# Two normalized convolution layers: prologue loads moved from SyncE's queue to GpSimd's, and memsets cut to the columns that stay

## The chip, the cores and the metric

The kernel runs on one core of a Trainium2 chip. A core has five engines that run side by side, each through its own instructions in order: TensorE (PE, matrix products), VectorE (DVE), ScalarE (ACT), GpSimd (POOL) and SyncE (SP). They meet through semaphores. DMA transfers between the chip's main memory (HBM) and the on-chip memory (SBUF) are issued by an engine and carried out by 16 DMA engines. In this kernel SyncE issues nearly all transfers, so its queue is a program of its own, in which a transfer that must wait holds back all that stand behind it.

The metric is the device time of one execution in microseconds. The kernel before takes 3223.17 us (median of 3 runs, 3222.82 to 3223.66).

## The reference

Input x has 4 images of 16 channels, 256 x 256, in float32. Two layers follow each other, and each adds its result to its input:

```python
# layer 0
h = group_norm(x)                                  # 8 groups of 2 channels, over H and W
logits = conv3x3(h, conv_w) + conv_b               # 16 -> 16*25 channels
w = softmax(logits.reshape(4, 16, 25, 256, 256), axis=2)
x = x + sum over the 25 offsets of (h shifted by the offset, zero outside) * w
# layer 1
g = group_norm(x)
base_w = base_weight.sum(axis=2)
spl_w  = (spline_weight * spline_scaler[..., None]).sum(axis=2)
x = x + conv3x3(silu(g), base_w) + conv3x3(b_splines(g), spl_w) + bias
```

So layer 0 is a 5 x 5 filter whose 25 weights differ at each pixel and channel and come from a 3 x 3 convolution. Layer 1 is a 3 x 3 convolution of nine functions of each value: silu and eight cubic B-splines.

## The kernel before, in words

The kernel has three stages.

**Prologue** (0 to about 132 us). It loads the 4 images, half an image (128 rows) at a time, 2 MB each (`load_x`, L408). The two halves of image 0 stay in SBUF (`held`), the other six go through three buffers (`xin`), so that a load waits until the half three before it has been read. For each half VectorE takes statistics (L519, L521), ScalarE squares it (`xq`, L528), and TensorE sums the squares over the channels (L531), which is for a bound on the logits. After both halves of an image, `group_stats` turns the statistics into mean and reciprocal deviation; the power -1/2 is taken on GpSimd (`rstd`, L152). Weights come in too: `wr` and `wnr` for layer 0 (L416 to L428), and for layer 1 `sw` (27 loads, L435), `ss` (3, L437) and `bw` (1, L442). `prepare0` sorts layer 0's weights into `wm` and `wp` (copies on GpSimd, L460 and L461). `prepare1` sums layer 1's weights (L483 to L498).

While images 1 to 3 are still being measured, image 0 is normalized: the generator `normalize` writes h to HBM in three layouts. `hs` holds rows in strips of 32 columns for the weighted sum. `hst` holds columns for the convolution's im2col, and `hsl` the same split into a rounded part and a rest (`hi` and `lo`). ScalarE makes the rows (`hsp`, L312, and `ht`, L325), TensorE transposes (L347), VectorE and ScalarE copy the transposed tiles out (`tt`, `hi`, `lo`, L340 to L355), and SyncE stores them (`put_rows` L273, `put_columns` L287). First of all `normalize` writes zeros around h: 4 stores to `hs` (L245) and 8 to `hst` and `hsl` (L251, L252). All of these are SyncE transfers, in the order in which the scheduler placed them: x loads, `wr`, `wnr`, then `sw`, `ss`, `bw`, the zeros, and only then the stores of h with the remaining x loads between them.

Tiles for `normalize` are made by `norm_tiles`, which zeroes them whole on GpSimd (L226, L228). What must be zero in them are only the borders: two columns at either side of `xp`, and the outermost column of `tt`, `hi` and `lo`. The rest is written over before it is read.

At the end of the prologue VectorE writes a flag that says whether the logits can't overflow, and each engine branches on it.

**Layer 0** (about 132 to 2290 us). A loop over 64 strips of 32 columns, each in steps of four columns: SyncE loads `am` and `an` (im2col of h, L628 and L638) and `u` (h's rows, L652). TensorE makes the logits (L775, L779), ScalarE the exponentials (L798), GpSimd multiplies by h (L803) and VectorE sums numerator and denominator (L680). `normalize` of the next image runs between the steps with tiles of its own, which `norm_tiles` zeroes again. The three `an` tiles are zeroed whole by VectorE first, and two of their rows (64 and 96) then set to one (L613, L615). Rows 64 and 96 carry the bias (its rounded part and the rest); rows 0 to 63 are loaded anew for each use, and the weights that rows 65 to 95 meet are zero.

**Layer 1** (about 2290 to 3222 us). ScalarE and VectorE evaluate the functions, TensorE convolves.

Two rules set the order of work around the change. Within the prologue a scheduler orders each engine's instructions. And transfers use eight completion counters in turn for each kind of issuing queue, so a transfer waits until the one eight before it has landed.

Of the kernel before, what the change touches and what calls it, by code (L numbers as in the profile page):

```python
# [11 lines left out]
F32 = mybir.dt.float32  # L12
# [21 lines left out]
def conv_preact_kernel(  # L34
# [12 lines left out]
    nc = tc.nc  # L47
    B, C, H, W = x.shape
# [3 lines left out]
    NH = H // P  # L52
# [3 lines left out]
    PAD = K // 2  # L56
# [10 lines left out]
    RP = P + 2  # L67
# [16 lines left out]
    hst = [[dram.tile([C, CT], F32, name=f"hst{b}_{h}") for h in range(NH)] for b in range(B)]  # L84
# [30 lines left out]
    KT = 6 * C + 1  # L115
# [17 lines left out]
    def group_stats(pool, psum, st, name):  # L133


        mv = pool.tile([P, G, 2], F32, name=f"mv_{name}", tag="mv")
        for g in range(G):
            nc.vector.bn_aggr(mv[:, g, :], st[:, g].rearrange("p n s -> p (n s)"))
        mps = psum.tile([P, G], F32, name=f"mps_{name}", tag="qp")
        nc.tensor.matmul(mps, lhsT=ones, rhs=mv[:, :, 0], start=True, stop=True)  # L140
        mean = pool.tile([P, G], F32, name=f"mean_{name}", tag="mean")
        nc.vector.tensor_copy(mean, mps)
        d = pool.tile([P, G], F32, name=f"d_{name}", tag="d")
        nc.vector.tensor_sub(d, mv[:, :, 0], mean)
        nc.vector.tensor_mul(d, d, d)
        nc.vector.tensor_add(d, d, mv[:, :, 1])
        vps = psum.tile([P, G], F32, name=f"vps_{name}", tag="qp")
        nc.tensor.matmul(vps, lhsT=ones, rhs=d, start=True, stop=True)
        var = pool.tile([P, G], F32, name=f"var_{name}", tag="var")
        nc.vector.tensor_scalar(var, vps, EPS, None, ALU.add)  # L150
        rstd = pool.tile([P, G], F32, name=f"rstd_{name}", tag="rstd")
        nc.gpsimd.tensor_tensor(rstd, var, mhalf, ALU.pow)  # L152
        return mean, rstd
# [63 lines left out]
    def norm_tiles(prep):  # L217


        xps = [prep.tile([P, QC, W + 2 * PAD], F32, name=f"xp{h}", bufs=1) for h in range(NH)]  # L220
        tts, his, los = [
            [prep.tile([P, NH, QG, RP], d, name=f"{v}{n}", bufs=1) for n in range(2)]
            for v, d in (("tt", F32), ("hi", F32R), ("lo", F32R))
        ]
        for t in (*tts, *xps):
            nc.gpsimd.memset(t, 0.0)  # L226
        for t in (*his, *los):
            nc.gpsimd.memset(t.bitcast(F32), 0.0)  # L228
        return prep, xps, tts, his, los

    zero = const.tile([PAD * C, max(RP, NST * SP)], F32, name="zero")
# [2 lines left out]
    zpad = const.tile([P, QC, PAD], F32, name="zpad")  # L234
    nc.vector.memset(zpad, 0.0)

    def normalize(b, ptr, tiles, held=None, copier=None):

        prep, xps, tts, his, los = tiles
        copier = copier or nc.scalar.copy
        for e in (0, HP - PAD):
            for r in range(PAD):
                nc.sync.dma_start(  # L245
                    hs[b][:, e + r].rearrange("s c w -> c s w"),
                    zero[0:C, 0 : NST * SP].rearrange("c (s w) -> c s w", s=NST),
                )
        for h in range(NH):
            for w in (0, (W + 1) * RP):  # L250
                nc.sync.dma_start(hst[b][h][:, w : w + RP], zero[0:C, 0:RP])  # L251
                nc.sync.dma_start(  # L252
                    hsl[b][h][:, :, w : w + RP].rearrange("c t r -> (c t) r"), zero[:, 0:RP]
                )

# [116 lines left out]
        for q in range(C // QC):  # L372
            ahead = rows(q + 1) if q + 1 < C // QC else iter(())
# [15 lines left out]
    with tc.tile_pool(name="prep0", bufs=2) as prep, tc.tile_pool(  # L389
# [5 lines left out]
    ) as pstat, tc.tile_pool(name="ptr0", bufs=3, space=PSUM) as ptr0:  # L395

        tiles = norm_tiles(prep)
        held = [pre.tile([P, C, W + 2 * PAD], F32, name=f"held{h}") for h in range(NH)]

        def load_x(n):  # L400
            b, h = divmod(n, NH)
            if b == 0:
                t = held[h][:, :, PAD : PAD + W]
                nc.gpsimd.memset(held[h][:, :, 0:PAD], 0.0)
                nc.gpsimd.memset(held[h][:, :, PAD + W :], 0.0)
            else:
                t = xin.tile([P, C, W], F32, name=f"xin_{n}", tag="xin")
            nc.sync.dma_start(t, x[b, :, h * P : (h + 1) * P, :].rearrange("c p w -> p c w"))  # L408
            return t
# [4 lines left out]
        for dj in range(3):  # L414
            v = conv_wt[dj].rearrange("(d c) n -> c d n", d=3)
# [5 lines left out]
        v = conv_wt[2, 2 * C : 3 * C]  # L421
# [8 lines left out]
        sw = pre.tile([P, 3, 9, nm], F32, name="sw")  # L430
        ss = pre.tile([P, 3, 9, nm], F32, name="ss")
        for d in range(3):
            dc = slice(d * C, (d + 1) * C)
            for k in range(9):
                nc.sync.dma_start(sw[:, d, k], spl_w[dc, k])  # L435
            v = spl_s[dc]
            nc.sync.dma_start(  # L437
                ss[:, d],
                bass.AP(tensor=v.tensor, offset=v.offset, ap=[v.ap[0], [0, NS], [1, 9 * nm]]),
            )  # L440
        bw = pre.tile([nm, 9, nm], F32, name="bw")
        nc.sync.dma_start(bw, base_w)  # L442

        ups = pstat.tile([P, 1], F32, name="ups", tag="hps")
        nc.tensor.matmul(
# [64 lines left out]
        ahead = iter(())  # L510
        for b in range(B):
            st = stat.tile([P, G, NH * (GC if b == 0 else 1), 6], F32, name=f"st0_{b}", tag=f"st0{min(b, 1)}")
            for hf in range(NH):
                n = b * NH + hf
                t = loaded.pop(0)
                for g in range(G):
                    if b == 0:
                        for k in range(GC):
                            nc.vector.bn_stats(st[:, g, hf * GC + k, :], t[:, g * GC + k, :])  # L519
                    else:  # L520
                        nc.vector.bn_stats(  # L521
                            st[:, g, hf, :],
                            t[:, g * GC : (g + 1) * GC, :].rearrange("p c w -> p (c w)"),
                        )
                    next(ahead, None)
                    next(ahead, None)

                nc.scalar.activation(xq, t, AF.Square)  # L528
                sq = pstat.tile([P, W], F32, name=f"sq_{n}", tag="sq")
                for c in range(C):  # L530
                    nc.tensor.matmul(  # L531
                        sq, lhsT=idr, rhs=xq[:, c], start=c == 0, stop=c == C - 1
                    )
                nc.vector.tensor_reduce(hm[:, n : n + 1], sq, AX.X, ALU.max)
                next(ahead, None)
                if n >= NH and n + 3 < B * NH:
                    loaded.append(load_x(n + 3))
            mean, rstd = group_stats(stat, pstat, st, f"x{b}")
            nc.vector.tensor_copy(nrm[b][:, 0], rstd)
            nc.vector.scalar_tensor_tensor(nrm[b][:, 1], mean, -1.0, rstd, ALU.mult, ALU.mult)  # L540
            ms = stat.tile([P, 2], F32, name=f"ms_{b}", tag="ms")
            nc.vector.tensor_mul(mean, mean, mean)
            nc.vector.tensor_reduce(ms[:, 0:1], mean, AX.X, ALU.add)
            nc.vector.tensor_scalar(ms[:, 0:1], ms[:, 0:1], 9.0 * GC, None, ALU.mult)
            nc.vector.tensor_reduce(ms[:, 1:2], rstd, AX.X, ALU.max)
            nc.vector.tensor_mul(ms[:, 1:2], ms[:, 1:2], ms[:, 1:2])
            v = hm[:, b * NH : (b + 1) * NH]
            nc.vector.tensor_scalar(v, v, 9.0 / 8.0, ms[:, 0:1], ALU.mult, ALU.add)
            nc.vector.tensor_scalar(v, v, ms[:, 1:2], None, ALU.mult)
            if b == 0:  # L550
                prepare0()
            if b == 1:
                prepare1()
            if b == 0:
                ahead = normalize(0, ptr0, tiles, held, nc.vector.tensor_copy)
                next(ahead)
        for _ in ahead:
            pass
# [39 lines left out]
    def layer0(shift):  # L598
# [4 lines left out]
        with tc.tile_pool(name=f"prep{arm}", bufs=2) as prep, tc.tile_pool(  # L603
# [5 lines left out]
        ) as plog, tc.tile_pool(name=f"prc{arm}", bufs=1, space=PSUM) as prc:  # L609
            ans = [imp.tile([KT, CI * RP], F32R, name=f"an{n}{arm}", bufs=1) for n in range(NIM)]  # L610
            for t in ans:
                v = t.bitcast(F32)
                nc.vector.memset(v, 0.0)  # L613
                for r in (4 * C, 6 * C):
                    nc.vector.memset(v[r : r + 1], 1.0)  # L615
            tiles = norm_tiles(prep)
            strips = [(b, hf, s) for b in range(B) for hf in range(NH) for s in range(NST)]
            nci = SW // CI
# [120 lines left out]
            ahead = iter(())  # L739
            for n, (b, hf, s) in enumerate(strips):  # L740
                if (hf, s) == (0, 0):
                    for _ in ahead:
                        pass
                    ahead = normalize(b + 1, ptr, tiles) if b + 1 < B else iter(())
# [12 lines left out]
                for j in range(0, SW, JG):  # L757
                    if j % CI == 0:
                        k = n * nci + j // CI
# [11 lines left out]
                    for j1 in range(0, JG, 2):  # L771
# [12 lines left out]
                        if shift:  # L784
                            mx = l0.tile([P, 2, C], F32, name=f"mx_{n}_{j}_{j1}{arm}", tag="mx")
                            for i in range(2):
                                v = lg[:, i, :NL].rearrange("p (m c d) -> p m c d", m=K, c=C)
# [3 lines left out]
                                w = bass.AP(  # L791
                                    tensor=mx.tensor, offset=mx.offset + i * C,
                                    ap=[mx.ap[0], [0, K], [1, C], [0, K]],
                                )
# [285 lines left out]
```

## Time and profile before

| what | value |
|---|---|
| time, median of 3 | 3223.17 us |
| prologue, to SyncE's last store of h | 0 to 132.2 us |
| its DMA traffic | 35.3 MB, mean 268 GB/s |
| busy over the whole span: DVE, PE, ACT, POOL | 96%, 89%, 69%, 60% |
| first product e*u of layer 0 (GpSimd) | 145.0 us |

The page's busy shares are over all three stages and hide the prologue, which is 4% of the span. It is best read by stretches: which engine is busy in it, and how much the DMA engines move. The DMA traffic of the prologue in 40 slices of 3.3 us (each digit is the busy share in tenths, below it GB/s):

```profile
DMA  0999999999512323241899999994999999999999
GB/s 5 324 350 348 349 349 348 349 348 348 157 30 38 97 41 91 40 122 26 260 257 348 347 371 284 347 314 182 354 366 297 349 342 365 335 368 332 372 375 376
```

The engines are full until slice 10, little used until slice 18 (about 60 us), and full again to the end.

### The profile page before, as it was taken

What the parts mean: (1) busy time and instruction counts of PE and PEld (TensorE: products, weight loads), DVE (VectorE), ACT (ScalarE), POOL (GpSimd) and SP (SyncE); (2) the same over time, 40 slices, a digit from 0 to 9 for tenths busy, and PEclk for the clock granted to TensorE, in tenths of its full rate; (3) what the DMA queues carried; (4) which work ended last, traced back from release to release, by engine and by line L of the source; (5) the groups of instructions that cost most, each with busy time, mean ns of one, the idle gap of its engine ahead of it and who ended that gap; (6) DMA issues with size and microseconds to landing.
All of it is one profiled execution on the core that took longest, in us unless ns stands there. A gap on an engine that the chain in (4) does not pass through costs nothing. (4 is left out here: it accounts for less than half of the span.)

```text
span 3222.0 us, 40428 instructions
## 1 busy us (share of the span) xinstructions
PE 2862.3 (89%) x14776; PEld 1490.7 (46%) x14776; DVE 3101.7 (96%) x1799; ACT 2208.0 (69%) x2233; POOL 1936.4 (60%) x659
## 2 busy tenths in 40 slices
PE   3499999999999999999999989859999989988988
PEld 3366665666566566656656656512222222222222
DVE  6589999999999999999999999999999999999997
ACT  6366555466554465554444444589999999999996
POOL 2299999999999999999999999900000000000000
PEclk7699999999999999999999999979999999999999
DMA  7988886778877788877756756678878778888883
GB/s 224 291 223 236 229 221 187 212 211 230 246 208 192 203 219 225 249 198 203 210 156 170 191 157 170 163 169 183 178 168 179 180 171 168 180 176 173 178 179 71
DMA packets 356531, 626.34 MB, mean 194 GB/s; under 512 B 45298, under 2 KB 222692, under 8 KB 340452
## 3 DMA queue, kind: packets, MB, share of 16 engines
q1 hardware_dynamic: 323300, 606.88, 75.3%
q10 hardware_dynamic: 33024, 16.78, 1.9%
q8 instruction: 121, 1.98, 0.3%
q14 instruction: 86, 0.70, 0.1%
HBM read 513.95 MB, written 104.24 MB: 192 GB/s over the span
## 5 line engine op out<-in xcount | busy, mean ns | idle before, releaser
L775 PE MATMUL lg<-wm,am 128*128 128x400 f32 x4096 | 1748.9, 508 | 123.4 <-ACT e L798 109.7
L803 POOL TENSOR_TENSOR e<-e,u 128x1600 f32<-128x1600 f32 x512 | 1789.1, 3536 | 68.5 <-ACT e L798 68.0
L680 DVE TENSOR_REDUCE nd<-e 128x128 f32<-128x3200 f32 x512 | 1747.5, 3477 | 23.3 <-POOL e L803 23.2
L798 ACT ACTIVATE e<-lg 128x800 f32<-128x800 f32 x1024 | 815.7, 836 | 896.5 <-DVE nd L680 768.9
L779 PE MATMUL lg<-wn,an 97*128 97x400 f32 x2048 | 1358.4, 663 | 0.5 <-DMA an<-hsl 0.5
L775 PEld LDWEIGHTS lg<-wm,am 128*128 128x128 f32 x4096 | 766.3, 194 | 450.1 <-ACT e L798 161.3
L961 PE MATMUL yp<-ring,wt 128*32 128x512 f32 x6144 | 755.1, 604 | 146.0 <-DVE ring L164 110.4
L779 PEld LDWEIGHTS lg<-wn,an 97*128 97x128 f32 x2048 | 390.8, 191 | 311.9 <-issue 15.6
L961 PEld LDWEIGHTS yp<-ring,wt 128*32 128x32 f32 x6144 | 206.5, 110 | 685.1 <-issue 477.9
L889 POOL MEMSET sx<- 16x256 f32 x8 | 2.4, 303 | 765.6 <-DMA out_dram<-yo 706.6
L977 PE MATMUL yp<-sl,ws 64*32 64x512 f32 x1536 | 176.5, 588 | 0.0
L164 DVE TENSOR_TENSOR ring<-ta,ta 128x2048 f32<-128x2048 f32 (+1 forms) x64 | 147.8, 2309 | 2.5
L164 DVE TENSOR_TENSOR ring<-tb,tb 128x2048 f32<-128x2048 f32 x64 | 145.6, 2276 | 2.6
L163 DVE TENSOR_TENSOR ta<-ta,ta 128x2048 f32<-128x2048 f32 (+1 forms) x64 | 147.3, 2301 | 0.0
L163 DVE TENSOR_TENSOR tb<-tb,tb 128x2048 f32<-128x2048 f32 x64 | 146.5, 2289 | 0.0
L908 ACT ACTIVATE sl<-sx,q 64x2048 f32<-64x2048 f32 x64 | 133.3, 2083 | 0.0
L160 ACT ACTIVATE ta<-ta 128x2048 f32<-128x2048 f32 (+1 forms) x64 | 122.3, 1911 | 0.0
L160 ACT ACTIVATE tb<-tb 128x2048 f32<-128x2048 f32 x64 | 120.5, 1883 | 0.6 <-POOL sx L889 0.6
L193 POOL TENSOR_TENSOR rstd<-rstd,mhalf 128x8 f32<-128x8 f32 x4 | 8.7, 2176 | 175.6 <-DVE rstd L191 175.6
L706 POOL TENSOR_TENSOR xc<-xc,nd 128x512 f32<-128x512 f32 x64 | 98.8, 1544 | 12.1 <-DVE nd L700 12.1
L977 PEld LDWEIGHTS yp<-sl,ws 64*32 64x32 f32 x1536 | 48.8, 106 | 116.2 <-issue 113.2
L923 ACT ACTIVATE xta<-xta,q 128x2048 f32<-128x2048 f32 (+2 forms) x44 | 91.6, 2083 | 0.0
(174 smaller groups left out, 2131.9 us busy)
## 6 DMA issues: line engine op xcount, KB each, us to landing
am<-hst SPq DMA_DIRECT2D x512, 194.6 KB
u<-hs SPq DMA_DIRECT2D x320, 288.0 KB
an<-hsl SPq DMA_DIRECT2D x512, 129.8 KB
xta<-x1s SPq DMA_DIRECT2D x40, 1024.0 KB
xtb<-x1s SPq DMA_DIRECT2D x40, 1024.0 KB
xtc<-x1s SPq DMA_DIRECT2D x40, 1024.0 KB
am<-hst SPq DMA_DIRECT2D x256, 129.8 KB
sx<-x1s SPq DMA_DIRECT2D x248, 128.0 KB
```

The lines of the kernel that those rows point to most:

```text
L160: nc.scalar.activation(s1, r1, AF.Square, scale=2.0)
L163: nc.vector.tensor_mul(s1, s1, r1)
L164: nc.vector.tensor_add(f, s2, s1)
L680: nc.vector.tensor_reduce(nd[:, :, j : j + JG, :], e.rearrange("p t j m c d -> p t j c m d"), AX.XY, ALU.add,)
L706: nc.gpsimd.tensor_sub(v, v, nd[:, 1].rearrange("p j c -> p c j"))
L775: nc.tensor.matmul(lg[:, i, :NL], lhsT=am[:, o : o + P], rhs=wm.rearrange("p m c d -> p (m c d)"), start=True, stop=False,)
L779: nc.tensor.matmul(lg[:, i, :NL], lhsT=an[:, o : o + P], rhs=wn.rearrange("p m c d -> p (m c d)"), start=False, stop=True,)
L798: nc.scalar.activation(ev, lg[:, :, :NL], AF.Exp)
L803: nc.gpsimd.tensor_tensor(e[:, 1].rearrange("p j m c d -> p j (m c) d"), e[:, 0].rearrange("p j m c d -> p j (m c) d"), uv, ALU.mult,)
L908: nc.scalar.activation(sl[n % 2][:, :, 1 : W + 1], t, AF.Silu, scale=sc[b][0][0 : RD * C], bias=sc[b][1][0 : RD * C],)
L961: nc.tensor.matmul(yp[t * M : (t + 1) * M], lhsT=wt[:, d, e].rearrange("p r o -> p (r o)"), rhs=ring[:, r0 + t * RT + d : r0 + t * RT + d ...
L977: nc.tensor.matmul(yp[t * M : (t + 1) * M], lhsT=ws[:, e].rearrange("p r o -> p (r o)"), rhs=sl[n % 2][:, t : t + NT + 1 : NT, e : e + W], ...
```

## The change

Three things are changed. (1) The loads of layer 1's weights (`sw`, `ss`, `bw`) and, for image 0 alone, the zeros around h are issued by GpSimd instead of SyncE. This is to free SyncE's queue for the stores of h and the x loads behind them. (2) `norm_tiles` zeroes only the border columns that no later write covers. (3) The `an` tiles are not zeroed and then given rows of ones; one memset sets rows 64 to 96 to one, since the loads cover rows 0 to 63 and the weights of rows 65 to 95 are zero. Parts 2 and 3 shorten GpSimd's and VectorE's memsets.

```diff
-        for t in (*tts, *xps):
-            nc.gpsimd.memset(t, 0.0)
-        for t in (*his, *los):
-            nc.gpsimd.memset(t.bitcast(F32), 0.0)
+        for t in xps:
+            nc.gpsimd.memset(t[:, :, 0:PAD], 0.0)
+            nc.gpsimd.memset(t[:, :, PAD + W :], 0.0)
+        for t in (*tts, *his, *los):
+            t = t if t.dtype == F32 else t.bitcast(F32)
+            nc.gpsimd.memset(t[:, 0, :, 0:1], 0.0)
+            nc.gpsimd.memset(t[:, NH - 1, :, RP - 1 :], 0.0)
...
-    def normalize(b, ptr, tiles, held=None, copier=None):
+    def normalize(b, ptr, tiles, held=None, copier=None, queue=nc.sync):
...
-                nc.sync.dma_start(
+                queue.dma_start(
                     hs[b][:, e + r].rearrange("s c w -> c s w"),
...
-                nc.sync.dma_start(hst[b][h][:, w : w + RP], zero[0:C, 0:RP])
-                nc.sync.dma_start(
+                queue.dma_start(hst[b][h][:, w : w + RP], zero[0:C, 0:RP])
+                queue.dma_start(
                     hsl[b][h][:, :, w : w + RP].rearrange("c t r -> (c t) r"), zero[:, 0:RP]
...
-                nc.sync.dma_start(sw[:, d, k], spl_w[dc, k])
+                nc.gpsimd.dma_start(sw[:, d, k], spl_w[dc, k])
             v = spl_s[dc]
-            nc.sync.dma_start(
+            nc.gpsimd.dma_start(
                 ss[:, d],
...
-        nc.sync.dma_start(bw, base_w)
+        nc.gpsimd.dma_start(bw, base_w)
...
-                ahead = normalize(0, ptr0, tiles, held, nc.vector.tensor_copy)
+                ahead = normalize(0, ptr0, tiles, held, nc.vector.tensor_copy, nc.gpsimd)
...
-                v = t.bitcast(F32)
-                nc.vector.memset(v, 0.0)
-                for r in (4 * C, 6 * C):
-                    nc.vector.memset(v[r : r + 1], 1.0)
+                nc.vector.memset(t.bitcast(F32)[4 * C : KT], 1.0)
```

## The prediction
> **What bounds the kernel now.** I read the page's 40 slices first: GpSimd and VectorE are full from slice 3 to about slice 28 (layer 0's loop), ScalarE and VectorE after it (layer 1). The diff touches neither loop; it touches the 132 us before them and the first 10 us of the loop. So the second view is busy time by stretch, cut at the points where the SyncE queue changes its work. Columns: stretch, length, busy time of each engine with its instruction count, granted clock, mean DMA share, GB/s.
>
> ```profile
> core 0: us, PE busy (x) PEld busy (x) DVE busy (x) ACT busy (x) POOL busy (x), PEclk, DMA share, GB/s
> 0.00:30.00 30.00, 9.67 (x42) 9.11 (x43) 24.83 (x77) 12.99 (x9) 9.95 (x22) 0.99 0.97 308
> 30.00:62.00 32.00, 18.45 (x81) 14.27 (x80) 20.73 (x64) 30.63 (x41) 7.10 (x13) 0.66 0.39 98
> 62.00:132.00 70.00, 20.95 (x95) 18.02 (x94) 43.79 (x123) 35.38 (x66) 3.28 (x2) 0.57 1.02 327
> ```
>
> The DMA engines are full, then idle six tenths of the time for 32 us, then full for 70 us. ScalarE is the reverse: 30.6 us busy of 32 in the hole, half idle after it. The timeline of the SyncE queue says why (start, length, queue, line, transfer, count):
>
> ```profile
> 35.89 5.70 SPq L435 DMA_DIRECT2D sw<-in_spl_w_dram  x9
> ...
> 56.72 1.85 SPq L245 DMA_DIRECT2D hs<-zero  x4
> ...
> 62.38 1.01 SPq L273 DMA_DIRECT2D hs<-hsp  x2
> 63.49 1.30 SPq L408 DMA_DIRECT2D xin<-in_x_dram  x1
> ```
>
> From 35.9 to 62.4 SyncE issues 43 small transfers, about 0.6 us each. Behind them stand the first stores of h (ready since 34.7 and 38.5, when ScalarE ended hsp) and the sixth x load (its buffer had been read by 33). The chain of waits up to 132 us shows who pays:
>
> ```profile
> DVE st L521 <- DMA xin<-in_x_dram: 13.3, 3, 8.6
> ...
> ACT xq L528 <- DMA xin<-in_x_dram: 11.2, 3, 4.8
> ...
> ACT hsp L312 <- DMA hs<-hsp: 4.9, 2, 4.2
> ```
>
> The x loads of batches 2 and 3 are late. The last one sets the end: its square is the row below at 108.1, and from there to SyncE's last put (131.6) it is a chain of statistics, flag and the last column tiles.
>
> ```profile
> 108.11 3.62 ACT L528 ACTIVATE xq<-xin 128x4096 fp32r<-128x4096 f32 x1 [4.18 <-DMA xin<-in_x_dram]
> ```
>
> GpSimd is idle for most of this, with two rows that matter:
>
> ```profile
> 28.79 1.66 POOL L152 TENSOR_TENSOR rstd_x<-var_x,mhalf 128x8 f32<-128x8 f32 x1 [19.49 <-DVE var_x L150]
> ```
> ```profile
> 30.82 0.87 ACT L312 ACTIVATE hsp<-held,nrm 128x576 f32<-128x576 f32 x1 [1.78 <-DVE ms L545]
> ```
>
> The reciprocal deviation of batch 0 runs on GpSimd the moment its variance is there, and 0.4 us later ScalarE starts normalizing. Everything ScalarE does from 30.8 on hangs on that row.
>
> **What the Trainium skill says.** (1) "DMA: Bandwidth & Descriptors", section "Issuing engines are not separate DMA queues": transfers of all issuing engines interleave on the same 16 DMA engines, so another issuer saves only issue time. No transfer of GpSimd's is in this trace, so it can't confirm that; but it shows issue time being the limit between 36 and 62 (DMA share 0.39). (2) "Perfetto Trace Analysis", section "DMA Instruction — SWDGE (GPSIMD)": a transfer issued by GpSimd has its descriptors written by GpSimd's own cores, and the instruction lasts until they are written. So an issue costs GpSimd engine time, in order with its other work. Not shown here. (3) "SBUF — State Buffer", section "Who interferes with whom": GpSimd and a VectorE copy in its two-port mode lock each other out. The trace agrees: the 16x128 copy of sel takes 6.23 us at 3.15, until GpSimd's memsets end near 9.3.
>
> **The change part by part.**
>
> Memsets at the start. Eight of 128x1040 took 7.4 us of GpSimd (1.75 to 9.05). Sixteen narrow ones replace them; the four 128x32 of held start 0.06 us apart, so about 1 us, and GpSimd is free at 3.0 instead of 9.3. By itself worth nothing: its next work was at 28.8, and the sel copy that it frees isn't needed until layer 1.
>
> Memsets at the start of layer 0. The eight on GpSimd (137.0 to 144.35) end before the first product e*u, which starts at 145.03 and waits 0.68 us for ScalarE. The nine of VectorE (130.0 to 140.5) become three; their only reader on the path, the an load at 135.55, had been waiting 0.3 us. VectorE's first reduce starts at 148.6, after the first product. Value: 0 to 0.3 us.
>
> SyncE's queue. Removed: 31 loads and 12 zero stores, 26.5 us of issue. The queue goes from wnr straight to the hs store. That store waits for the landing of the transfer eight before it on SyncE's rotating completion counters, the fifth x load; that landed at about 35.9, and now shares the DMA engines with the moved loads. These took 8 us of full DMA time in the hole (share 0.31 and 0.33 over 40 to 60, and a little either side), so I take 43. The first store can go at 43 instead of 62.4.
>
> GpSimd's queue, the cost. In the changed program's instruction order, GpSimd issues 27 sw, 3 ss, bw, 4 hs and 1 hst, 36 transfers, *ahead of* the batch 0 reciprocal. Waiting behind them: the reciprocal, then all of ScalarE's normalizing, then SyncE's stores. The trace doesn't show what one such issue costs. Below: SyncE's own rows, 0.597 us for sw, 0.46 for hs zeros, 0.43 for a 16-row one. Above: the 2.0 us fixed cost of a whole GpSimd transfer ("DMA: Bandwidth & Descriptors", section "Anatomy of one DMA — SWDGE (gpsimd) path"), which would hold only if nothing overlapped. I take SyncE's rows scaled by 1.0/0.6, the ratio of first-byte latencies that the same page gives for the two paths ("Latency and other measured facts"): an estimate of 1.0 us for 128-row transfers, 0.77 and 0.72 for the zeros. Waits for the transfer eight before hardly bind at that rate, as eight issues last 8 us.
> 31 x 1.0 + 4 x 0.77 + 0.72 = 34.8; from 3.0 that is 37.8; plus 1.66 for the reciprocal and 0.4 to ScalarE: normalizing starts at 39.9, not 30.8, 9.1 us late.
> What else queues: seven zeros (5.0), sw*ss (2.97), the copies to wm and wp (2.1) end near 49.6. ScalarE's cast of wp comes some 17 us of its work after 39.9, so that hides.
>
> Now the end. ScalarE was busy 55.7 us between 30.8 and the last square at 108.1 (30.6 in the hole, about 25 from 62 on) and waited 21 us, mostly for what SyncE issued late. With SyncE open those waits go. I leave 4 us of them, twice the rate of the hole (1.4 in 32). Last square: 39.9 + 55.7 + 4 = 99.6, 8.5 earlier. Its x load is there: from the first hs store to its issue took 36.4 us (62.4 to 98.8) and 9.3 to land; from 44 that is 89.7. DMA work also fits: the full 70 us from 44 end at 114, while the prologue would end at 131.6 - 8.5 = 123. The loops behind it only shift. Rounding off 0.3 us for slower x loads in the first 40 us: 3223.2 - 8.2 = 3215.
>
> **The rivals.** All hang on the same unknown, c, the issue time of a 128-row transfer on GpSimd.
> A. Forecast, c near 1.0: 3215.
> B. Cheap issue, c of 0.6 to 0.75: the reciprocal is hardly late (24 to 29), and the DMA engines become the bound; end at 114 to 116, 16 us saved: 3207. For it: the transfers are tiny (24 KB). Against it: software writes their descriptors.
> C. Cancels, c near 1.25: normalizing starts at 48.6, the last square at 108.3: 3223. For it: the same arithmetic with one number a quarter larger. Against: zeros with few rows are likely cheaper.
> D. The other side: a new wait takes the place of the old one. At c = 1.5, 52.2 us of issue, start at 57.3, last square at 117, 9 us later: 3232. At 2.0: 69.6, 74.7, 134: 3249. For it: every batch's reciprocal is on GpSimd, and the x loads fill the DMA engines until 36, so landings may be slow and the eight-counter wait may bind. Against: SyncE's x loads leave room between packets if the queues take turns.
>
> **How the numbers follow.** A 0.42, B 0.20, C 0.18, D 0.20. Predicted time is A's. The range leaves out the cheapest end of B and most of D past c = 1.6: 3205 to 3234. Faster than 3216.7: B and seven tenths of A, 0.49. Within 0.2%: the rest of A and most of C, 0.29. Slower than 3229.6: D and a sliver of C, 0.22.
>
> **What would show it.** In the changed kernel's timeline: GpSimd's queue issuing sw from about 3 us at about 1 us each; the first reciprocal near 38 rather than 28.8 and waiting for the queue, not for VectorE; the first hs store near 44; the sixth x load right behind it; the last square near 100; DMA share above 0.8 between 44 and 120; the first logits near 130 instead of 138.9. I am wrong if the reciprocal is after 48 (D), if it is before 32 (B), or if the last square stays near 108 while the reciprocal is early, since then ScalarE's waits were not SyncE's doing.

## The result and the profile after

| kernel | median, us | lowest to highest | runs |
|---|---|---|---|
| before | 3222.99 | 3222.45 to 3223.66 | 4 |
| changed | 3209.85 | 3207.31 to 3210.43 | 4 |

The ratio is 0.9958, 95% interval 0.994 to 0.9975: 13.1 us faster, where 8.2 were forecast. A later series gave 0.9962 (0.9948 to 0.9975). Line numbers move by one to three: L435 of before is L438 here, L528 is L531.

Busy time by stretch of the changed kernel, with the cuts of the prediction's first view (columns as there):

```profile
core 0: us, PE busy (x) PEld busy (x) DVE busy (x) ACT busy (x) POOL busy (x), PEclk, DMA share, GB/s
0.00:30.00 30.00, 8.22 (x36) 7.84 (x36) 16.30 (x70) 11.51 (x9) 20.62 (x65) 0.86 0.97 286
30.00:62.00 32.00, 17.64 (x70) 12.72 (x70) 27.79 (x75) 28.49 (x46) 12.08 (x21) 0.61 0.82 256
62.00:132.00 70.00, 31.09 (x132) 24.93 (x133) 42.28 (x123) 40.16 (x66) 5.34 (x19) 0.61 1.01 324
```

The hole between 30 and 62 us is mostly gone: the DMA engines move 256 GB/s in it instead of 98. ScalarE does nearly as much there as before (28.5 us busy, 30.6 before), so it was not ScalarE that made the hole. The timeline of SyncE's queue shows what became of it:

```profile
42.47 1.02 SPq L276 DMA_DIRECT2D hs<-hsp  x2
43.59 1.34 SPq L411 DMA_DIRECT2D xin<-in_x_dram  x1
58.03 0.36 SPq L276 DMA_DIRECT2D hs<-hsp  x1
...
63.74 0.89 SPq L411 DMA_DIRECT2D xin<-in_x_dram  x1
...
83.30 0.63 SPq L411 DMA_DIRECT2D xin<-in_x_dram  x1
```

The first stores of h go at 42.5 instead of 62.4, and the last three x loads at 43.6, 63.7 and 83.3 instead of 63.5, 77.1 and 98.8. SyncE's last store of h is issued by 117.3 us instead of 132.2, 14.9 earlier, and the first `am` load of layer 0 stands at 118.9 instead of 133.6. A gap is left between 45 and 58 us, in which SyncE waits for one thing. The waits up to 125 us, first of SyncE's own queue and then of the other engines (us in total, times, longest):

```profile
SPq L276 <- ACT hsp L325: 13.0, 1, 13.0
```
```profile
ACT xq L531 <- DMA xin<-in_x_dram: 5.0, 1, 5.0
...
DVE st L524 <- DMA xin<-in_x_dram: 2.3, 1, 2.3
```

Waiting for loads into `xin` fell from 13.3 to 2.3 us on VectorE and from 11.2 to 5.0 us on ScalarE. What is left belongs to the third x load, near 27.8 us; behind the hole neither engine's waits name an x load any more. ScalarE's timeline has the first normalizing and the last square, which no longer waits:

```profile
34.47 0.87 ACT L315 ACTIVATE hsp<-held,nrm 128x576 f32<-128x576 f32 x1 [2.98 <-DVE ms L548]
...
93.62 3.61 ACT L531 ACTIVATE xq<-xin 128x4096 fp32r<-128x4096 f32 x1
```

And GpSimd's queue, which the forecast hung on:

```profile
2.50 4.40 POOL L438 DMA_DIRECT2D sw<-in_spl_w_dram  x8
8.22 0.52 POOL L438 DMA_DIRECT2D sw<-in_spl_w_dram  x1 [1.32 <-DMA sw<-in_spl_w_dram]
...
29.78 0.51 POOL L254 DMA_DIRECT2D hst<-zero  x1 [0.45 <-DMA sw<-in_spl_w_dram]
32.42 1.68 POOL L152 TENSOR_TENSOR rstd_x<-var_x,mhalf 128x8 f32<-128x8 f32 x1 [2.12 <-DVE var_x L150]
```

One issue takes 0.52 us, not 1.0. The first eight go without a wait; the ninth is held until a transfer ahead of it has landed (1.32 us here), and such waits go on to the end of the queue. The 36 transfers end at 30.29, so (30.29 - 2.50) / 36 = 0.77 us each, of which 0.52 is issue and 0.25 waiting. Then the reciprocal waits 2.12 us for its variance, and not for the queue.

### The profile page after: what moved, and what is told of

Same layout as the page of the kernel before. It is cut to its first block, busy times and chain, and to the rows that moved or that the text cites. A ratio compares the mean times of both kernels' runs of the same rounds, so it can differ in the third digit from the quotient of the medians.

```text
span 3205.4 us, 40450 instructions
## 1 busy us (share of the span) xinstructions
PE 2891.0 (90%) x14776; PEld 1505.6 (47%) x14776; DVE 3091.9 (96%) x1793; ACT 2206.5 (69%) x2233; POOL 1946.5 (61%) x718
## 3 DMA queue, kind: packets, MB, share of 16 engines
q8 instruction: 121, 1.98, 0.3%
## 5 line engine op out<-in xcount | busy, mean ns | idle before, releaser
L962 PE MATMUL yp<-ring,wt 128*32 128x512 f32 x6144 | 783.2, 625 | 117.9 <-DVE ring L164 81.3
L780 PEld LDWEIGHTS lg<-wn,an 97*128 97x128 f32 x2048 | 391.0, 191 | 311.8 <-issue 14.6
L962 PEld LDWEIGHTS yp<-ring,wt 128*32 128x32 f32 x6144 | 221.5, 113 | 670.1 <-issue 473.2
```

The source lines that it names most:

```text
L780: nc.tensor.matmul(lg[:, i, :NL], lhsT=an[:, o : o + P], rhs=wn.rearrange("p m c d -> p (m c d)"), start=False, stop=True,)
L962: nc.tensor.matmul(yp[t * M : (t + 1) * M], lhsT=wt[:, d, e].rearrange("p r o -> p (r o)"), rhs=ring[:, r0 + t * RT + d : r0 + t * RT + d ...
```

## The experiments

Theory at the start: the gain is SyncE's freed queue alone; the size was missed through the price of an issue on GpSimd; and what is left at the end is ScalarE's stream, which runs nearly without a pause from 34.5 us to the last square. The rival took the DMA engines for the bound. There were three series, with five or more runs of each kernel; each series has its own runs of the kernel before (3224.0, 3221.94 and 3222.72 us), and gains are against these. The changed kernel itself ran again only in the third series. For kernels of the first two, a gain within 2 us of its 13 can't be told from it.

**One part alone.** Part 1 without the new memsets (e1), the new memsets without part 1 (e2):

```diff
 e1, against the changed kernel
-        for t in xps:
-            nc.gpsimd.memset(t[:, :, 0:PAD], 0.0)
...
+        for t in (*tts, *xps):
+            nc.gpsimd.memset(t, 0.0)
...
 e2, against the kernel before: the same lines the other way round
```

> The loads of layer 1's weights and the zeros of image 0 on GpSimd's queue, all memsets as before. Theory of the queue: the whole gain comes from SyncE's queue being free; the whole-tile memsets only make GpSimd start to issue near 9.3 us instead of 2.5, and 31 loads at 0.77 us each (the rate in the changed kernel) end near 33, so that the first reciprocal starts near 33 to 34 instead of 32.4. Time 3209 to 3212, as the changed kernel or 1 us more. Rival, the memsets carry part of the gain (7 us of GpSimd at the start, 8 us of VectorE at the start of layer 0): 3215 or more.

> Only the memsets cut, all transfers on SyncE as before. Theory of the queue: nothing on the path moves, 3223 within 1 us; the first product e*u starts at 145 within 0.5 us. Rival, the memsets carry part of the gain: 3215 to 3219.

Measured: e1 3209.14 us (ratio 0.9953, 0.9939 to 0.9967), e2 3223.81 (0.9999, 0.9991 to 1.0008). The whole gain comes with the move to GpSimd's queue; the memsets are worth nothing that can be measured, though in e2 GpSimd is busy 1.98 us of the first 10 instead of 8.73.

**Half of the squares.** Images 1 to 3 are squared and summed on 8 of 16 channels, which takes 10.6 us from ScalarE in the first 130 us (68.41 busy instead of 79.05). The bound on the logits then leaves out half the channels.

```diff
-                nc.scalar.activation(xq, t, AF.Square)
+                cs = C if b == 0 else C // 2
+                nc.scalar.activation(xq[:, 0:cs], t[:, 0:cs], AF.Square)
```

> As the changed kernel, but the squares of images 1 to 3 and the sums of them on TensorE take 8 of 16 channels: this leaves out half of the channels in the bound on the logits. Each square on ScalarE drops from 3.6 to 1.8 us; four of them lie between the start of normalizing and the last square. If ScalarE is the bound of the prologue now, the last square starts 7 us earlier (near 86.5) and the time is 3200 to 3203. Rival, the DMA engines are the bound (share 1.0 from 60 us on): the last square waits for its x load, gain 0 to 3 us, 3207 to 3210.

Measured: 3208.8 us (0.9951, 0.9937 to 0.9964), 15.2 gained where the changed kernel gained 13.1 and 12.8; the intervals overlap. The theory of ScalarE's stream, which asked for 3200 to 3203, falls. The last square of this kernel stands nearly where it stood (92.9 instead of 93.6), and now waits for its x load:

```profile
92.93 1.91 ACT L532 ACTIVATE xq<-xin 128x2048 fp32r<-128x2048 f32 x1 [1.68 <-DMA xin<-in_x_dram]
```

A stream without pauses is not yet a bound: with less to do, ScalarE only waited more.

**Zeros back on SyncE.** The loads stay on GpSimd.

```diff
-                ahead = normalize(0, ptr0, tiles, held, nc.vector.tensor_copy, nc.gpsimd)
+                ahead = normalize(0, ptr0, tiles, held, nc.vector.tensor_copy)
```

> As the changed kernel, but the twelve zero stores go back to SyncE, where they stand ahead of the first store of h: 12 issues of 0.43 to 0.46 us, first store of h at 48 instead of 42.5. If ScalarE's instruction stream behind the first reciprocal is the bound, the 5.6 us hide, since SyncE waits 13 us for ScalarE after the sixth x load: 3209 to 3211. Rival, the moment at which SyncE is free for h sets the end: 5.6 us more, 3215.

Measured: 3218.67 us (0.9983, 0.9975 to 0.9991). It gained 5.3 us where the changed kernel gained 13.1. I had expected almost no loss, and the rival 5.6 us; it is about 8. The 12 zeros cost SyncE 5.5 us. With them came another order of the instructions, which the scheduler makes anew for each kernel; the two effects weren't tried apart. SyncE, GpSimd and ScalarE of this kernel:

```profile
42.40 1.75 SPq L248 DMA_DIRECT2D hs<-zero  x4
...
47.96 1.01 SPq L276 DMA_DIRECT2D hs<-hsp  x2
...
66.96 0.36 SPq L276 DMA_DIRECT2D hs<-hsp  x1
```
```profile
31.50 2.96 POOL L486 TENSOR_TENSOR sw<-sw,ss 128x1296 f32<-128x1296 f32 x1 [5.04 <-DMA ss<-in_spl_s_dram]
34.42 1.67 POOL L152 TENSOR_TENSOR rstd_x<-var_x,mhalf 128x8 f32<-128x8 f32 x1
```
```profile
60.86 3.62 ACT L531 ACTIVATE xq<-xin 128x4096 fp32r<-128x4096 f32 x1 [0.67 <-ACT ht L328]
64.38 2.37 ACT L315 ACTIVATE hsp<-held,nrm 128x576 f32<-128x576 f32 x3
```

The zeros hold the first stores of h back by 5.5 us (47.96 against 42.47). GpSimd has sw*ss ahead of the reciprocal (2 us later), and ScalarE two squares ahead of the third piece of rows instead of one. The third store goes at 67.0, 8.9 us later than 58.0, and the end moves by the same 9 us (first `am` load 127.9 against 118.9).

**A second theory.** The traces of these four kernels, of before and of the changed kernel have one sum in common. The end is taken as the first `am` load. From 10 us to it I took stretches of 10 us and added up what their DMA share lacks to 1 (the changed kernel: 2.0 at 40, 4.6 at 50, 0.8 at 70, 7.4 in all); a share above 1 counts as no lack. The end less this idle time was the same within 1.2 us in all six. The theory made of it: *the prologue ends when the DMA engines' work is done, and that takes their work plus the time they were left idle.* The other runs test it.

**Where the loads stand, and in which queue.** In e5 the 31 weight loads stay on GpSimd, but behind the reciprocal and the copies of wm and wp. In e7 SyncE issues them, behind the 6th x load. In e8 they are left out.

```diff
 e5: forced behind the last GpSimd instruction of prepare0
+                load_weights()
 e7: nc.sync instead of nc.gpsimd, and
+                if n == 2:
+                    load_weights()
 e8
-                nc.gpsimd.dma_start(sw[:, d, k], spl_w[dc, k])
...
+        for t in (sw, ss, bw):
+            nc.gpsimd.memset(t, 0.01)
```

> Changed kernel, with layer 1's 31 weight loads still on GpSimd's queue but placed behind image 0's reciprocal and the copies of wm and wp (about 37 us instead of 7 us). Theory (the end of the prologue is the DMA engines' work plus the time they stand idle; in the changed kernel 7 us are left idle between 40 and 60 us): the x loads share the engines with nothing, the third x load lands near 24.5 us again, the reciprocal starts near 29 instead of 32.4 us, and the small transfers fall into the idle stretch: 3203 to 3206 us, DMA share over 0.85 in 40 to 60 us. Rival (normalizing's chain from the reciprocal sets the end, at a fixed distance): 3206 us. Rival (the small loads collide with wr, wnr and the 6th x load instead): 3209 to 3212 us.

> Changed kernel, with layer 1's 31 weight loads issued by SyncE again, but behind the 6th x load instead of ahead of the first stores of h; the zeros stay on GpSimd. It asks whether the queue counts or the place in it. 31 loads at 0.6 us hold SyncE for 18.6 us from about 40 us. Theory (idle DMA time): the loads fall into SyncE's own wait for the third piece of rows and into the idle stretch, the reciprocal is back near 29 us, the third store and the 7th x load go near 60 to 63 us: 3206 to 3211 us. Rival (any loads left on SyncE cost what they cost before): 3216 to 3223 us.

> Changed kernel without layer 1's 31 weight loads: sw, ss and bw are set to a constant on GpSimd instead, so layer 1's weights are left out. The zeros stay on GpSimd. It prices what the loads still cost on their new queue. Theory (idle DMA time): about 6 us of the engines' work are gone ahead of the reciprocal, which starts near 29 us; the idle stretch of 40 to 60 us stays: 3202 to 3205 us. Rival (fixed distance from the reciprocal): 3206 us. Rival (the new queue hides them wholly): 3209 to 3210 us.

Measured: e5 3207.38 us (0.9955, 0.9942 to 0.9969), e7 3216.14 (0.9981, 0.9974 to 0.9988), e8 3204.95 (0.9946, 0.9932 to 0.9959). GpSimd in e5 and then in e8, SyncE in e7:

```profile
29.50 1.68 POOL L152 TENSOR_TENSOR rstd_x<-var_x,mhalf 128x8 f32<-128x8 f32 x1 [18.54 <-DVE var_x L150]
...
38.58 4.75 POOL L443 DMA_DIRECT2D sw<-in_spl_w_dram  x9
```
```profile
28.74 1.68 POOL L152 TENSOR_TENSOR rstd_x<-var_x,mhalf 128x8 f32<-128x8 f32 x1 [11.80 <-DVE var_x L150]
```
```profile
40.30 10.48 SPq L443 DMA_DIRECT2D sw<-in_spl_w_dram  x9
...
65.46 0.37 SPq L276 DMA_DIRECT2D hs<-hsp  x1
```

e8 says what the moved loads still cost. Without them the reciprocal is at 28.74, as before the change (28.79), instead of 32.42. The 3.6 us of delay come from the third x load, which shares the DMA engines with the loads. It belongs to image 1, but VectorE has its first statistics ahead of image 0's variance in its order, and gets to them at 27.8 in the changed kernel, after a wait of 2.3 us for the load, and at 24.4 before the change, without a wait. And the end less the idle time falls by 7, about what the 31 loads take of the engines. e5 gives the reciprocal back (29.5), yet gains at most 2 us over the changed kernel and misses the 3203 to 3206 that I had expected: the idle time is the same (7.1 us), now in three places (shares of 0.76 from 30, 0.77 from 50 and 0.76 from 70 us). An earlier chain alone moves the end little. e7 and e5 have the loads in nearly the same stretch (40 to 65 and 39 to 59 us), on different queues, and differ by 8.8 us in one series: on SyncE the third store of h stands behind them until 65.5 (54.0 in e5). So at this place it is the queue that counts. I had expected 3206 to 3211 for e7, as I took 0.6 us per load; the first nine took 1.16 each.

**A longer queue on GpSimd.** e4 issues each sw load twice, so that 58 loads stand ahead of the reciprocal, as the prediction feared of a dear issue.

```diff
                 nc.gpsimd.dma_start(sw[:, d, k], spl_w[dc, k])
+                nc.gpsimd.dma_start(sw2[:, d, k], spl_w[dc, k])
```

> Changed kernel with each of the 27 sw loads issued twice on GpSimd, the second time into a tile that nothing reads: 58 loads stand ahead of image 0's reciprocal. It does what the prediction feared of a slow queue. At the 0.77 us per transfer that the changed kernel showed, the reciprocal comes near 47 us instead of 32.4. The scheduler puts the 6th and 7th x loads ahead of the first stores of h. Theory (the end is the DMA engines' work plus their idle time): the x loads fill the time before the stores, so the end moves by the added 6 us of work and a few us of idle time only: first load of am at 125 to 130 us, 3216 to 3221 us. Rival (fixed distance from the reciprocal to the end): 15 us later than the changed kernel, 3225 us. Rival (the queue is hidden anyway): 3210 us.

Measured: 3218.8 us (0.9987, 0.998 to 0.9994), first `am` load at 127.1.

```profile
45.65 1.69 POOL L152 TENSOR_TENSOR rstd_x<-var_x,mhalf 128x8 f32<-128x8 f32 x1
```

The reciprocal comes 13.2 us later and the end 7.8 later (against 119.4 in the same series): 2.4 more of work (114.0 - 111.6) and 5.3 more of idle time. The fixed distance from the reciprocal is refuted in this direction too: the x loads, which went ahead of the stores here, filled part of the delay.

**Filling the gap.** Three attempts on the idle stretch of 40 to 60 us: a fourth x buffer (e9), the stores of rows on GpSimd's queue (e11), the stores of rows issued ten steps after their copies instead of four, so that the first columns go ahead of the third one (e12).

```diff
 e9
-        name="xin", bufs=3
+        name="xin", bufs=4
...
 e11, in put_rows
-            nc.sync.dma_start(
+            queue.dma_start(
 e12
-                        moves.append((4, partial(put_rows, q, h, hsp)))
+                        moves.append((10 if b == 0 else 4, partial(put_rows, q, h, hsp)))
```

> Changed kernel with four x buffers instead of three, so that the 6th x load is issued ahead of wr and the 7th where the 6th was. Theory (idle DMA time): 5.9 us of x load move from behind the idle stretch of 40 to 60 us into it: 3203 to 3206 us. Rival (ScalarE's stream, which in the changed kernel runs without a pause from 34.5 us to the last square's end at 97 us): no gain, 3209 to 3212 us.

> The changed kernel as it is, for comparison with the other three: 3209 to 3211 us; first load of am near 119 us; 7 us of idle DMA time between 40 and 110 us.

> Changed kernel with image 0's stores of rows (hs) on GpSimd's queue too, so that SyncE holds only x loads and stores of columns behind its first loads. In the changed kernel the columns of the first piece are ready near 51 us and stand behind the third store of rows, which waits until 58 us. Theory (idle DMA time): the stretch 50 to 60 us fills by up to 5 us: 3204 to 3208 us. Rival (GpSimd's stores of rows wait for ScalarE and hold up the reciprocals of images 1 to 3 behind them, or ScalarE's stream is the bound): 3209 to 3214 us.

> Changed kernel in which image 0's stores of rows are issued ten steps after their copies instead of four: on SyncE the six stores of columns of the first piece now stand ahead of the third store of rows. Theory (idle DMA time): as the run before, the stores of columns go near 51 us instead of 58.5: 3204 to 3207 us. Rival (ScalarE's stream is the bound, or hsp's two buffers come free later and hold it up): 3209 to 3213 us.

Measured: e9, in the second series, 3212.18 us (0.9967, 0.9955 to 0.998); in the third the changed kernel again 3209.97 (3209.50 to 3211.51), e11 3206.83 (3206.49 to 3208.01; 0.9952, 0.9939 to 0.9966), e12 3209.07 (3207.56 to 3210.75; 0.9959, 0.9945 to 0.9972). The stretch from 50 to 60 us in the changed kernel, e11 and e12:

```profile
50.00:60.00 10.00, 7.10 (x31) 5.16 (x30) 7.09 (x29) 9.97 (x18) 1.66 (x1) 0.67 0.54 174
```
```profile
50.00:60.00 10.00, 4.29 (x14) 2.45 (x14) 5.77 (x15) 7.56 (x13) 2.19 (x6) 0.50 0.89 312
```
```profile
50.00:60.00 10.00, 7.10 (x33) 5.40 (x31) 7.37 (x30) 9.97 (x18) 1.66 (x1) 0.67 0.97 328
```

Both fill it (share 0.89 and 0.97 instead of 0.54). e11 brings the first `am` load from 119.4 to 116.0 and beats the changed kernel by 3.1 us without an overlap of their runs. In e12 most of what was filled opens again behind it (a share of 0.88 from 60 to 70 us and 0.67 from 110 us to the end, where the changed kernel has 1.02 and 1.03), and its 0.9 us are inside the spread; the 3204 to 3207 that I had expected was missed. e9 missed too: the 6th x load moved ahead of wr as meant, but this put wr and all stores of h later. SyncE and the stretch behind:

```profile
19.13 16.46 SPq L411 DMA_DIRECT2D xin<-in_x_dram  x2
35.64 7.27 SPq L419 DMA_DIRECT2D wr<-in_conv_wt_dram  x3
...
48.44 1.03 SPq L276 DMA_DIRECT2D hs<-hsp  x2
...
67.09 0.36 SPq L276 DMA_DIRECT2D hs<-hsp  x1
```
```profile
60.00:70.00 10.00, 6.06 (x20) 4.15 (x20) 9.23 (x31) 9.37 (x15) 0.55 (x1) 0.59 0.21 67
```

The gap wasn't filled but moved, from 50 to 60 us to 60 to 70.

All runs in one table (us). Idle: what the DMA share lacks to 1 in stretches of 10 us, from 10 us to the first `am` load. Gain: against before in the same series, from medians; the other columns are of one profiled execution each.

| kernel | gain | first am load | idle | am less idle |
|---|---|---|---|---|
| before | | 133.6 | 21.3 | 112.3 |
| changed | 13.1 | 118.9 | 7.4 | 111.5 |
| changed, again (e10) | 12.8 | 119.4 | 7.8 | 111.6 |
| e1 issuers alone | 14.9 | 118.1 | 5.7 | 112.4 |
| e2 memsets alone | 0.2 | 134.1 | 21.4 | 112.7 |
| e3 zeros on SyncE | 5.3 | 127.9 | 16.0 | 111.9 |
| e4 loads doubled | 3.9 | 127.1 | 13.1 | 114.0 |
| e5 loads behind | 14.6 | 117.5 | 7.1 | 110.4 |
| e6 half of the squares | 15.2 | 118.8 | 7.2 | 111.6 |
| e7 loads late on SyncE | 5.8 | 125.2 | 15.2 | 110.0 |
| e8 no weight loads | 17.0 | 114.7 | 10.1 | 104.6 |
| e9 four x buffers | 9.8 | 121.1 | 10.3 | 110.8 |
| e11 rows on GpSimd | 15.9 | 116.0 | 5.1 | 110.9 |
| e12 rows later | 13.7 | 117.7 | 5.9 | 111.7 |

The last column stays between 110.0 and 112.7 unless the work itself is changed: 7 less without the loads, 2.4 more with 27 added. The change took 13.9 us of idle time out of 21.3, and the end came 14.6 earlier. Behind the prologue nothing regular is lost or gained: from the first `am` load to their end the profiled executions took 3088.4 to 3092.6 us, before 3090.3.

The column has to be read with care. It is nearly the time for which the engines were busy, so it must come out alike wherever the same bytes are moved at the same rate, and alone it doesn't say what the end waits for. There is also a rival for which no run was made: the prediction's own chain, from the last square to the end at a fixed distance. In 12 of the 14 profiles the first `am` load stands 24.9 to 25.9 us behind the last square (25.4 before, 25.3 in the changed kernel), e4 and e8 among them. Only e9 and e11 part the two. The last square in e9 and in e11:

```profile
85.21 3.61 ACT L531 ACTIVATE xq<-xin 128x4096 fp32r<-128x4096 f32 x1
```
```profile
96.90 3.62 ACT L531 ACTIVATE xq<-xin 128x4096 fp32r<-128x4096 f32 x1 [3.92 <-PE sq L534]
```

In e9 it is 8.4 us earlier than in the changed kernel and the end 2.2 later; in e11 it is 3.3 later and the end 2.9 earlier. So an early last square isn't enough, and the sum holds in both (110.8 and 110.9). The other runs fit both readings. In e12 the DMA engines stand half idle near the end (0.47 from 110 to 114 us), so there the end waits for more than their work. And the sum doesn't tell which edit will lower the idle time: e3 and e9 were misjudged on that.

## Why the prediction was right, and where it was not

- *SyncE's 43 small transfers make the hole, and late x loads the end.* The first half is right, and shown: e1 alone has the whole gain, e7 loses more than half of it with the loads on SyncE again. The second fits this kernel, whose end stays 25.3 us behind the last square (25.4 before), but not as a rule: in e9 the last x loads came earlier and the end later.
- *Memsets worth nothing by themselves.* Right (e2). The sel copy fell from 6.23 to 0.21 us, hidden as said.
- *First hs store at 43.* Right: 42.47, 6th x load right behind. But the sign of a DMA share above 0.8 from 44 us on failed (0.54 from 50 to 60): the sum had no term for SyncE's 13 us of waiting for ScalarE behind that load.
- *c, 1.0 us per issue on GpSimd.* This term of the sum was mis-sized. It measured 0.52, below the lower bound that I had taken from SyncE's row (0.597). I had scaled SyncE's issue by the ratio of first-byte latencies in the Trainium skill ("DMA: Bandwidth & Descriptors", "Latency and other measured facts"). A latency says when data starts to move, not how long the issuing engine is held, and GpSimd's rows show only the second.
- *Waits for the transfer eight before hardly bind.* Wrong at the real rate: 36 x 0.52 = 18.7 us of issue took 27.8, so about 9 were waits. In sum the queue ended at 30.3 and not at 37.8.
- *Reciprocal at 37.8, waiting for the queue.* It came at 32.42, just above the 32 that would have meant rival B, and waited for VectorE. The delay that there is, 3.6 us, comes through the shared DMA engines (e8, e5). The skill's sentence on them ("Issuing engines are not separate DMA queues"), which I cited and priced at 0.3 us, is borne out here.
- *55.7 us of work and 4 us of waits to the last square.* Predicted 59.7, measured 93.62 - 34.47 = 59.15. So the last square came 14.5 us earlier instead of 8.5, and the 6 us between are 5.4 from the start of normalizing and 0.5 here. That the stretch came out within 0.5 was luck. Its parts were off: the work before was 54.2 us (30.6 + 23.6, not 25), and 4 us of waits are about one and a half times the hole's rate (1.4 in 32), not twice; after the change it was 53.1 us of work and 6.0 of waits. And as a rule it fails: a reciprocal 13.2 us later moved the end by 7.8 (e4), and one 3 us earlier by 2 at most (e5).
- *What bounds it after.* I let ScalarE's chain set the end and noted that DMA work "also fits". The runs speak for the reverse: the DMA engines are nearly full from 60 us to the end (shares of 0.92 to 1.08), and taking 10.6 us from ScalarE gains 2 us at most (e6). Rival B had this mechanism, with its cheap issue and DMA bound, and 3207; I gave it 0.20. It missed 3209.85 by 2.9 us, and it had no term for the idle stretch left between 40 and 60 us. In the forecast's own sum the price c is most of what 3215 lacks in gain, but that sum hung on a bound that e6 doesn't bear out.
- *Rivals C and D.* The arithmetic for a dear queue was too dark as well: e4 starts normalizing at 51.4 us, between C's 48.6 and D's 57.3, where they put the time at or above that of before, and is still 3.9 us faster than before.

## What to carry to other kernels

When a short stretch has DMA shares near 1 on both sides of a hole, add up the holes. Here the end moved by what an edit took out of them, to within 2.5 us, in all runs that kept the same transfers; an engine that looks busy throughout may just be following. Check then that the engines stay full to the very end, and look for a run in which the sum and the last chain of waits part. Look for the transfer at the head of the queue that everything else stands behind (here 31 loads and 12 zeros, then one store of rows that waited 13 us), and move what is ready past it, to another queue if that one has room. Before an issue on a new queue is priced, ask for three numbers apart: how long the issuing engine is held, how soon the completion counters come round, and what the bytes take from transfers that are already on the path.

## What the runs showed of the hardware

- A 24 KB load of 128 rows holds GpSimd 0.52 us (0.54 by the median of the changed kernel's 27 rows) and SyncE 0.60 (the median in the kernel before; nine take 5.70 us, 0.63 each with the gaps). Beside the x loads it lands 5.9 us after its issue from GpSimd (median of 27), so that eight counters allow one per 0.74 us, near the 0.77 measured.
- A 576 KB store of rows held GpSimd 0.89 to 0.96 us (e11).
- VectorE's scaling of a 128x2 tile took 0.21 us in e1, and 3.59 in the changed kernel, until GpSimd's product beside it ended (40.58 and 40.54). VectorE and then GpSimd:

```profile
36.99 3.59 DVE L551 TENSOR_SCALAR hm<-hm,ms 128x2 f32<-128x2 f32 x1
```
```profile
37.59 2.95 POOL L486 TENSOR_TENSOR sw<-sw,ss 128x1296 f32<-128x1296 f32 x1
```

  That one shuts the other out agrees with the skill's "SBUF — State Buffer" ("Who interferes with whom"); the product itself isn't slower than in e1 (2.94 us). That page gives the shared ports to whichever comes first. VectorE's row begins 0.6 us ahead here and is held all the same; GpSimd was issuing transfers without a break until 37.57, and who came first stays open. What the 3.4 us are worth wasn't tried by itself: e1, without them, has its end 0.8 us earlier.
